# The first sequence normalized in groups of one, one and two token tiles, and the first nine loads on one queue

## The chip, the cores and the metric

The kernel runs on one core of a Trainium2 chip. A core has a matrix engine (TensorE, PE in the profile), a vector engine (VectorE, DVE), a scalar engine (ScalarE, ACT), a general engine (GpSimd, POOL) and a sync engine (SyncE, SP) that here only issues transfers between the device memory and the on-chip buffers. Each engine works through its own list of instructions in order and waits for the others by semaphores. The metric is the time of one execution in device microseconds, lower is better; it is given as the median of several runs.

## The reference, cut to what matters

Four sequences of 512 tokens with 256 features pass through a gated linear scan ("attention") and then through six feed-forward blocks. The computation is in float32.

```python
def _layernorm(x, axis=-1, eps=1e-05):
    m = jnp.mean(x, axis=axis, keepdims=True)
    v = jnp.var(x, axis=axis, keepdims=True)
    return (x - m) / jnp.sqrt(v + eps)

def _L0_attn_ref(x, Wq1, Wq2, Wk1, Wk2, Wv, Wo, norm_w):
    q = jax.nn.silu(x @ Wq1 @ Wq2)        # 256 -> 128 -> 512
    log_f_raw = x @ Wk1 @ Wk2             # 256 -> 128 -> 512
    v = x @ Wv                            # 256 -> 512
    f = jax.nn.sigmoid(log_f_raw)
    a = jnp.exp(jax.nn.log_sigmoid(f))
    k = 1.0 - a
    _, h = jax.lax.associative_scan(combine, (a, k * v), axis=1)   # h_t = a_t h_(t-1) + k_t v_t
    out = q * h
    out = out * jax.lax.rsqrt(jnp.mean(out * out, axis=-1, keepdims=True) + EPS) * norm_w
    return out @ Wo                       # 512 -> 256

# six blocks, the last without the layer norm behind it
h = jax.nn.gelu(jnp.einsum('bsd,hd->bsh', x, w1) + b1, approximate=False)   # 256 -> 1024
x = jnp.einsum('bsh,dh->bsd', h, w2) + b2 + x                               # 1024 -> 256
x = (x - mu) * jax.lax.rsqrt(var + LN_EPS) * g + b

# the whole
x = L0_attn_x                                             # (4, 512, 256)
x = x + _layernorm(attention(_layernorm(x)))
x = x + _layernorm(ffn(_layernorm(x)))
```

## The kernel before, in words

**Tiles.** A sequence is four token tiles of 128 tokens (rows) by 256 features. The products want the features on the partitions, so a normalized token tile is transposed: for each of the two halves `d` of the 256 features one transpose per token tile. For the first two sequences PE does it against the identity (`transpose`, L547; `to_features`, L714) into one of two PSUM tiles `pt`, which ACT copies to the on-chip memory. The later sequences pass through DRAM instead (`passage`, L748: DVE transposes blocks of 32, SP stores the block, and four reads, L744, bring it back in the other order).

**Stages.** For each sequence: layer norm; features; `k1_q1` (L835), which multiplies by Wk1 and Wq1 to two results of 128 x 512; then for each of four quarters `e` of the 512 value features `value(e)` (L840, the product with Wv) and `scan(e)` (L845: products of `k1` and `q1` with quarters of Wk2 and Wq2, sigmoids on ACT, the scan itself on DVE, the product with q on POOL). The output product of one sequence (`output`) is mixed into the scans of the next. Behind the attention come six feed-forward blocks for two groups of two sequences, whose products are computed from sums of blocks of the weights and inputs that POOL forms.

**The first sequence.** Its tiles are normalized in two groups of two tiles (`first_norm`, L789): statistics on DVE (`token_stats`, L673, two instructions, L678 and L679), an add and a power of -0.5 on POOL for the two tiles together (`rstd_of`, L683, recorded as L520 and L508), then subtract and multiply on DVE (`centred`, L707, recorded as L520). `first_features` (L810) transposes a group's two tiles for each `d` and copies 128 x 256 to the on-chip memory. `projected` (L819) then makes its products group by group, so that k1, q1 and value of the first sequence consist of products with 256 columns each, where later sequences have 512.

**Warming.** Before any data is there, PE multiplies a tile of ones by itself (`warm`, L587) into a PSUM bank that nothing reads: six products of 256 columns at once (`WARM`, L592), and two more of 128 columns (`FILL`, L1292) that are tied to the second normalized tile `one.n[1]`.

**Loads.** The token tiles of the first sequence go out alternately on SP's and ACT's queue (L599), Wk1 and Wv on ACT's, Wq1, Wk2 and Wq2 on SP's. Sequence 1's tiles, the norm weights, Wo, the other sequences and the first feed-forward weights follow on SP's. Transfers take their completion semaphores from a set of eight in turn, so a transfer waits until the one eight places before it has landed.

**Order.** Nothing but the start (the warming products, the constants) is issued in the order of the text. Each operation is recorded with an engine, an estimated cost and its dependencies (`Plan.op`, L269). `Plan.latest` (L290) gives each one a due time, counted back from the end along PE's work, and `Plan.run` (L308) simulates the engines: each takes, of what is ready by the estimated times, the operation that is due first. The order that comes out is fixed in the program. A change in costs or dependencies at the start can thus shift the order on any engine further on.

Of the kernel before, what the change touches and what calls it, by code (L numbers as in the profile page):

```python
# [16 lines left out]
P = 128  # L17
# [9 lines left out]
POOLROWS = (2,)  # L27
AFTER = 6.0
LAST_WAYS = "POOL POOL ACT DVE DVE".split()
WARM = 6  # L30
FILL = 2


# [112 lines left out]
def lines_of(text):  # L146
    return [line.split() for line in text.strip().split("\n")]


class View:  # L150


    def __init__(self, bufs, ap, turns):
        self.bufs, self.ap, self.turns = bufs, ap, turns
# [103 lines left out]
class Plan:  # L258
# [6 lines left out]

    def __init__(self):
        self.ops = []

    def op(self, engine, cost, emit, reads, writes, wire=None):  # L269
        n, deps = len(self.ops), set()  # L270
        for v in (*reads, *writes):
            assert v.turns == tuple(b.turn for b in v.bufs), "taken by another"
        for b in (b for v in reads for b in v.bufs):
            deps.add(b.writer)
            b.readers.append(n)
        for b in (b for v in writes for b in v.bufs):
            deps.add(b.writer)
            deps.update(b.readers)
            b.writer, b.readers = n, []
        self.ops.append((engine, cost, emit, deps - {n, None}, wire))  # L280
# [9 lines left out]
    def latest(self):  # L290

        last = [1e9] * len(self.ops)
        at = sum(cost for engine, cost, *_ in self.ops if engine == "PE")
        end = at + AFTER
        for n in reversed(range(len(self.ops))):
            engine, cost, _, deps, _ = self.ops[n]
            if engine == "PE":
                at = min(at - cost, last[n])
                last[n] = at
            elif last[n] == 1e9:  # L300
                last[n] = end
            for d in deps:
                a = self.ops[d]
                took = a[1] + (2.0 + a[4] if a[4] else 0.0)
                last[d] = min(last[d], last[n] - self.lag(d, n) - took)
        return last

    def run(self):  # L308
# [45 lines left out]
def kernel(  # L354
# [30 lines left out]
    NB, _, HID = w1t.shape  # L385
    NT = S // P
    ND = E // P
# [11 lines left out]
    plan = Plan()  # L399

    def tiles(name, shape, n=1, pool=sb):
        return [
            Buf(pool.tile(shape, F32, tag=f"{name}{k}", name=f"{name}_{k}"))
            for k in range(n)
        ]
# [7 lines left out]
    xs = [[Buf(v.ap[:, ts(t, E)]) for t in range(NT)] for v in x_of]  # L413
# [35 lines left out]
    txs = [Buf(tx_of.ap[:, ts(k, 2 * P)]) for k in range(len(lines_of(B_SUMS)))]  # L449
# [29 lines left out]
    mvs = Ring([tiles(f"mv{k}", [P, NT, 2], 1)[0] for k in range(8)])  # L479
    rs = Ring(tiles("r", [P, 4, NT], 8))  # L480
# [20 lines left out]
    def tt(engine, dst, a, b, alu):  # L501
        cost = 0.14 + 0.00213 * dst.size if engine == "POOL" else 0.07 + 0.00104 * dst.size
        if alu == ALU.pow:
            cost = 0.29 + 0.18 * dst.size
        plan.op(
            engine,
            cost,
            lambda: on(engine).tensor_tensor(dst.ap, a.ap, b.ap, alu),  # L508
            [a, b],
            [dst],  # L510
        )

    def tscalar(engine, dst, src, s0, s1, op0, op1=None):
        by = [s.ap if isinstance(s, View) else s for s in (s0, s1)]
        kw = {} if op1 is None else {"op1": op1}
        cost = 0.15 + 0.003 * dst.size if engine == "POOL" else 0.07 + 0.001 * dst.size
        plan.op(
            engine,
            cost,
            lambda: on(engine).tensor_scalar(dst.ap, src.ap, *by, op0, **kw),  # L520
            [src, *(s for s in (s0, s1) if isinstance(s, View))],
            [dst],
        )
# [23 lines left out]
    def transpose(dst, src):  # L547
        plan.op(
            "PE",
            0.107,  # L550
            lambda: nc.tensor.transpose(dst.ap, src.ap, ident.ap),
            [src],
            [dst],
        )

    def load(dst, src, engine="SP"):
        queue = nc.sync if engine == "SP" else nc.scalar
        kept = isinstance(src, View)
        plan.op(
            engine,  # L560
            0.45,
            lambda: queue.dma_start(out=dst.ap, in_=src.ap if kept else src),
            [src] if kept else [],
            [dst],
            dst.size * P * 4 / 0.26e6,
        )
# [17 lines left out]
    nothing, unread = txs[-1], banks.free[-1]  # L584
    nc.vector.memset(nothing.ap, 1.0)

    def warm(n):  # L587
        nc.tensor.matmul(
            unread.ap[:, :n], nothing.ap[:, :P], nothing.ap[:, :n], start=True, stop=True
        )  # L590

    for _ in range(WARM):  # L592
        warm(2 * P)
# [2 lines left out]
    nc.vector.memset(ones.ap, 1.0)  # L596

    nc.scalar.activation(sts.bufs[0].ap[:, :1], ones.ap, AF.Sigmoid)
    for t in range(NT):  # L599
        load(xs[0][t], x[0, ts(t, P), :], ("SP", "ACT")[t % 2])  # L600
    load(wk1_s, wk1.rearrange("(c p) h -> p c h", p=P), "ACT")
    load(wq1_s, wq1.rearrange("(c p) h -> p c h", p=P))
    load(wv_s, wv.rearrange("(c p) f -> p c f", p=P), "ACT")
    load(wk2_s, wk2)
    load(wq2_s, wq2)

    def load_x(b):
        for t in range(NT):
# [74 lines left out]
    def rstd_of(mv, to, of=None, lo=0, hi=NT, negative=True):  # L683

        ve, r, nm, nb = (to[:, k, lo:hi] for k in range(4))
        if of is None:
            tscalar("POOL", ve, mv[:, lo:hi, 1], LN_EPS, None, ALU.add)
        else:
            tt("POOL", ve, of[:, lo:hi], mv[:, lo:hi, 1], ALU.add)
        tt("POOL", r, ve, neg_half[:, lo:hi], ALU.pow)  # L690
        if not negative:
            return r
        tscalar("POOL", nm, mv[:, lo:hi, 0], -1.0, None, ALU.mult)
        tt("POOL", nb, nm, r, ALU.mult)
        return r, nb
# [11 lines left out]
    def centred(src, mv, r, t, t0):  # L707

        z = nns.next()
        by = mv[:, t, 0:1], r[:, t - t0 : t - t0 + 1]  # L710
        tscalar("DVE", z, src, *by, ALU.subtract, ALU.mult)
        return z

    def to_features(srcs, d, xt, scale=None, bias=None):  # L714


        pt = pts.next()[:, : len(srcs) * P]
        for t, src in enumerate(srcs):
            transpose(pt[:, ts(t, P)], src[:, ts(d, P)])
        if scale is None:  # L720
            act(xt, pt)
        else:
            act(xt, pt, AF.Identity, bias, scale)
# [48 lines left out]
    class Attention:  # L772
# [14 lines left out]
                self.there = passage(self.n, early)  # L787

        def first_norm(self):  # L789
            self.n = []  # L790
            for lo in range(0, NT, 2):
                mv = mvs.next()
                for t in (lo, lo + 1):
                    token_stats(mv, xs[self.b][t], t)
                r = rstd_of(mv, rs.next(), lo=lo, hi=lo + 2, negative=False)
                for t in (lo, lo + 1):
                    self.n.append(centred(xs[self.b][t], mv, r, t, lo))
            self.xt = []

        def features(self, d):  # L800
            xt = tcs.next()
# [5 lines left out]
            if d == ND - 1:  # L807
                early.back(self.there)

        def first_features(self, half):  # L810

            for d in range(ND):
                xt = txs[2 * half + d][:]
                to_features(self.n[2 * half : 2 * half + 2], d, xt)
                if half == 0:
                    self.xt.append([])
                self.xt[d].append(xt)

        def projected(self, w):  # L819

# [460 lines left out]
    att = [Attention(b) for b in range(B)]  # L1281
    att[0].first_norm()
    for e in range(NE):
        tscalar("POOL", wo_s[e], wo_s[e], nw_s[:, e : e + 1], None, ALU.mult)
    att[0].first_features(0)
    att[0].first_features(1)
    for b in range(B):
        one = att[b]
        past = att[b - 1] if b else None
        one.k1_q1()  # L1290
        if b == 0:
            for _ in range(FILL):  # L1292
                plan.op("PE", 0.43, lambda: warm(P), [one.n[1]], [unread])
        if b + 1 < B:
            att[b + 1].norm()
        if b >= 2:
            att[b - 2].ffn_norm(early)
        one.value(0)
        one.scan(0)
        one.value(1)  # L1300
        if past:
            past.output(0)
        one.scan(1)
        if past:
            past.output(1)
        one.value(2)
        if past:
            past.output(2)
        one.scan(2)
        if past:  # L1310
            past.output(3)
        one.value(3)
        if past:
            past.residual()
        if b >= 2:
            att[b - 2].ffn_input(0)
        if b + 1 < B:
            att[b + 1].features(0)
        one.scan(3)
        if b >= 2:  # L1320
            att[b - 2].ffn_input(1)
        if b + 1 < B:
            att[b + 1].features(1)
# [7 lines left out]
    for i in range(NB):  # L1331
        for g in range(NG):
            last, hidden = output, Hidden(i, g)
# [105 lines left out]
```

## Time and profile before

| what | value |
| --- | --- |
| median of 3 runs | 685.31 us (685.26 to 686.22) |
| the profiled execution's own time | 685.2 us |
| its span, first to last instruction | 683.4 us |
| mean granted TensorE clock over the span | 0.998 |
| PE busy | 671.9 us (98%) |
| DVE, ACT, POOL busy | 469.7, 357.8, 531.9 us |
| moved by DMA | 73.74 MB, mean 108 GB/s |
| PE's first matmul | 1.17 us after the span's start |
| PE's first transpose of a normalized tile | 6.68 us |
| PE's last matmul ends | 676.8 us |

The profile shows one execution. A line names an engine, a source line, an operation, output<-inputs by the program's names, the shape, how many (xN), and times; what stands in brackets or behind an arrow is the idle time ahead of it and what ended it. "PE" are matmuls, "PEld" weight loads, which lie beside them. A float32 product appears as two matmul rows. Since many operations are recorded by a helper, one line number can stand for many places: L540 is any product, L551 any transpose, L508 any tensor-tensor operation on DVE or POOL, L491 and L493 activations and copies on ACT. "SPq" and "ACTq" rows are the issue of a transfer, not the transfer.

### The profile page before, as it was taken

The numbers are of one execution on the slowest core, as the hardware profiler recorded it, in microseconds if no ns is written. First come the engines' busy times: TensorE is split into PE (matmuls) and PEld (weight loads), VectorE is DVE, ScalarE is ACT, GpSimd is POOL, SyncE is SP. The second block draws the span as 40 slices with busy tenths as digits, with TensorE's granted clock in tenths as the row PEclk, the third lists the DMA queues.
The fourth block names the chain that finished last, engine by engine and source line by source line (L and its number), as shares of the span: only waits on it lengthen the run. The fifth ranks groups of instructions, "written<-read, shape, count | busy, mean of one in ns | idle before, by whom it ended". The sixth has DMA issues, their size and how long they took to land.

```text
span 683.4 us, 8266 instructions
## 1 busy us (share of the span) xinstructions
PE 671.9 (98%) x2384; PEld 443.6 (65%) x2384; DVE 469.7 (69%) x902; ACT 357.8 (52%) x623; POOL 531.9 (78%) x692
## 2 busy tenths in 40 slices
PE   8999999999999999999999999999999999999995
PEld 7565568747658568467476585584674765855885
DVE  5567666866938839759569478387495694793955
ACT  3847757725734636437257346364472482463731
POOL 4997769858988668996589886589866798875764
PEclk9999999999999999999999999999999999999999
DMA  8401312143262141440431631414514306316511
GB/s 253 165 1 62 123 62 80 45 154 92 88 204 78 55 161 43 181 154 24 153 94 62 216 92 64 151 35 175 162 32 153 93 1 195 112 56 185 153 40 62
DMA packets 81838, 73.74 MB, mean 108 GB/s; under 512 B 6272, under 2 KB 70784, under 8 KB 81792
## 3 DMA queue, kind: packets, MB, share of 16 engines
q1 hardware_dynamic: 80672, 72.02, 32.6%
q10 hardware_dynamic: 1120, 1.18, 0.6%
q8 instruction: 19, 0.31, 0.2%
q14 instruction: 27, 0.22, 0.1%
HBM read 43.82 MB, written 29.36 MB: 107 GB/s over the span
## 4 chain that ended last, share of the span: by engine, by line
PE 66%; DVE 17%; POOL 8%; ACT 4%; issue 4%; DMA 0%; DVEq 0%; POOLq 0%; ACTq 0%
PE bank L540 60%; DVE ht L508 9%; POOL tc L508 5%; PE pt L540 5%; DVE tmp L508 3%; DVE st L678 2%; ACT ht L491 2%; DVE tc L508 1%; ACT tmp L493 1%; POOL tx L508 1%; DVE mv L679 1%; POOL r L508 1%; POOL r L520 1%; ACT bank L491 0%; DMA x<-in_x 0%
## 5 line engine op out<-in xcount | busy, mean ns | idle before, releaser
L540 PE MATMUL bank<-tx,sa 128*128 128x256 f32 x672 | 163.1, 380 | 1.7 <-ACT tmp L493 1.5
L493 ACT COPY tmp<-bank 128x512 f32<-128x512 f32 x144 | 83.8, 583 | 135.9 <-PE bank L540 127.1
L540 PEld LDWEIGHTS bank<-tx,sa 128*128 128x128 f32 x672 | 126.2, 190 | 28.6 <-issue 7.8
L508 POOL TENSOR_TENSOR tc<-ht,tc 128x512 f32<-128x512 f32 x96 | 123.8, 1300 | 26.8 <-ACT bank L491 22.5
L491 ACT ACTIVATE ht<-ht,b 128x512 f32<-128x512 f32 x156 | 106.9, 715 | 12.6 <-DVE ht L508 12.6
L508 DVE TENSOR_TENSOR ht<-tmp,bank 128x512 f32<-128x512 f32 x156 | 101.3, 679 | 17.5 <-ACT tmp L493 12.5
L540 PE MATMUL bank<-tc,w 128*128 128x512 f32 (+1 forms) x216 | 95.2, 578 | 0.0
L508 DVE TENSOR_TENSOR tmp<-tmp,bank 128x512 f32<-128x512 f32 x96 | 64.4, 677 | 40.2 <-PE bank L540 23.3
L540 PE MATMUL bank<-tc,sb 128*128 128x512 f32 (+2 forms) x208 | 88.2, 560 | 0.9
L540 PE MATMUL bank<-ht,sb 128*128 128x512 f32 (+2 forms) x208 | 88.0, 555 | 0.0
L530 DVE SCALAR_TENSOR_TENSOR tmp<-bank,b,xt 128x512 f32<-128x512 f32 (+1 forms) x52 | 36.4, 700 | 74.7 <-PE bank L540 74.7
L540 PE MATMUL bank<-ht,w 128*128 128x512 f32 (+1 forms) x200 | 83.0, 567 | 0.0
L508 POOL TENSOR_TENSOR tx<-xt,tx 128x256 f32<-128x256 f32 x108 | 75.8, 733 | 1.0
L540 PEld LDWEIGHTS bank<-tc,sb 128*128 128x128 f32 x208 | 38.5, 190 | 47.1 <-issue 35.4
L540 PEld LDWEIGHTS bank<-tc,w 128*128 128x128 f32 x216 | 40.7, 190 | 39.9 <-issue 36.1
L508 POOL TENSOR_TENSOR tx<-xt 128x256 f32<-128x256 f32 x24 | 17.4, 727 | 60.0 <-ACT xt L491 50.8
L540 PEld LDWEIGHTS bank<-ht,w 128*128 128x128 f32 x200 | 37.9, 190 | 38.1 <-issue 31.8
L491 ACT ACTIVATE n<-x,r 128x256 f32<-128x256 f32 x90 | 47.7, 587 | 26.7 <-POOL r L508 26.7
L540 PEld LDWEIGHTS bank<-ht,sb 128*128 128x128 f32 x208 | 39.0, 190 | 33.7 <-issue 30.6
L508 DVE TENSOR_TENSOR tmp<-bank,tmp 128x512 f32<-128x512 f32 (+2 forms) x54 | 35.4, 655 | 36.1 <-PE bank L540 27.4
L540 PE MATMUL bank<-tx,w 128*128 128x256 f32 x224 | 56.8, 379 | 0.0
L540 PE MATMUL bank<-xt,w 128*128 128x256 f32 x192 | 51.4, 379 | 0.0
(94 smaller groups left out, 1019.2 us busy)
## 6 DMA issues: line engine op xcount, KB each, us to landing
x<-passed SPq DMA_DIRECT2D x120, 128.0 KB, 2.9
passed<-x SPq DMA_DIRECT2D x16, 512.0 KB, 2.7
passed<-x SPq DMA_DIRECT2D x28, 256.0 KB, 2.5
room<-passed SPq DMA_DIRECT2D x56, 128.0 KB, 3.1
w<-in_w1t SPq DMA_DIRECT2D x6, 1024.0 KB, 5.0
w<-in_w2t SPq DMA_DIRECT2D x6, 1024.0 KB, 5.7
passed<-room SPq DMA_DIRECT2D x16, 256.0 KB, 2.2
passed<-room SPq DMA_DIRECT2D x6, 512.0 KB, 2.7
```

The lines of the kernel that those rows point to most:

```text
L491: lambda: nc.scalar.activation(dst.ap, src.ap, func, **kw)
L493: else nc.scalar.copy(dst.ap, src.ap),
L508: lambda: on(engine).tensor_tensor(dst.ap, a.ap, b.ap, alu),
L520: lambda: on(engine).tensor_scalar(dst.ap, src.ap, *by, op0, **kw),
L530: lambda: nc.vector.scalar_tensor_tensor(dst.ap, a.ap, by, b.ap, op0, op1),
L540: lambda: nc.tensor.matmul(dst.ap, lhs.ap, rhs.ap, start=start, stop=True, skip_group_check=True),
L678: nc.vector.bn_stats(st.ap, src.ap)
L679: nc.vector.bn_aggr(mv.ap[:, t, :], st.ap)
```

## The change

The norm and features of the first sequence go in groups of one, one and two tiles; the products of its first two tiles have 128 columns each instead of 256 for both. The fillers hang on the first normalized tile instead of the second. There are five warming products instead of six. The first nine loads all go out on SP's queue, in an order that is written down (their due times are set to very early values, in that order), and no load is left on ACT's queue.

```diff
-WARM = 6
+WARM = 5
+FIRST = ((0,), (1,), (2, 3))
 FILL = 2
@@ class Plan
     def __init__(self):
         self.ops = []
+        self.first = 0
@@ latest
                 last[d] = min(last[d], last[n] - self.lag(d, n) - took)
+        last[: self.first] = [n - 1e9 for n in range(self.first)]
         return last
@@ loads
-    for t in range(NT):
-        load(xs[0][t], x[0, ts(t, P), :], ("SP", "ACT")[t % 2])
-    load(wk1_s, wk1.rearrange("(c p) h -> p c h", p=P), "ACT")
-    load(wq1_s, wq1.rearrange("(c p) h -> p c h", p=P))
-    load(wv_s, wv.rearrange("(c p) f -> p c f", p=P), "ACT")
-    load(wk2_s, wk2)
-    load(wq2_s, wq2)
+    firsts = [
+        (xs[0][0], x[0, ts(0, P), :]),
+        (xs[0][1], x[0, ts(1, P), :]),
+        (wk1_s, wk1.rearrange("(c p) h -> p c h", p=P)),
+        (wq1_s, wq1.rearrange("(c p) h -> p c h", p=P)),
+        (xs[0][2], x[0, ts(2, P), :]),
+        (xs[0][3], x[0, ts(3, P), :]),
+        (wv_s, wv.rearrange("(c p) f -> p c f", p=P)),
+        (wk2_s, wk2),
+        (wq2_s, wq2),
+    ]
+    for dst, src in firsts:
+        load(dst, src)
+    plan.first = len(firsts)
@@ first_norm
-            self.n = []
-            for lo in range(0, NT, 2):
-                mv = mvs.next()
-                for t in (lo, lo + 1):
+            self.n, self.xt = [], [[] for _ in range(ND)]
+            for group in FIRST:
+                mv, lo = mvs.next(), group[0]
+                for t in group:
                     token_stats(mv, xs[self.b][t], t)
-                r = rstd_of(mv, rs.next(), lo=lo, hi=lo + 2, negative=False)
-                for t in (lo, lo + 1):
+                r = rstd_of(mv, rs.next(), lo=lo, hi=group[-1] + 1, negative=False)
+                for t in group:
                     self.n.append(centred(xs[self.b][t], mv, r, t, lo))
-            self.xt = []
@@ first_features
-        def first_features(self, half):
-            for d in range(ND):
-                xt = txs[2 * half + d][:]
-                to_features(self.n[2 * half : 2 * half + 2], d, xt)
-                if half == 0:
-                    self.xt.append([])
-                self.xt[d].append(xt)
+        def first_features(self):
+            for k, group in enumerate(FIRST):
+                for d in range(ND):
+                    xt = txs[ND * k + d][:, : len(group) * P]
+                    to_features([self.n[t] for t in group], d, xt)
+                    self.xt[d].append(xt)
@@ the start of the program's body
-    att[0].first_features(0)
-    att[0].first_features(1)
+    att[0].first_features()
...
-                plan.op("PE", 0.43, lambda: warm(P), [one.n[1]], [unread])
+                plan.op("PE", 0.43, lambda: warm(P), [one.n[0]], [unread])
```

## The prediction

> **What bounds the kernel now.** I read the page first, then the waits of TensorE, the chain of waits in order of time, and the timeline of the first 14 us. The page:
>
> ```profile
> PE 671.9 (98%) x2384; PEld 443.6 (65%) x2384; DVE 469.7 (69%) x902; ACT 357.8 (52%) x623; POOL 531.9 (78%) x692
> ```
>
> TensorE (PE) is busy for all but 11.5 us of 683.4, so the time is its start, its work, its few gaps and a tail. The waits of PE over the span show the two gaps of the start (1.2 us, then 0.6 us for the first normalized tile):
>
> ```profile
> PE bank L588 <- DVE ones L596: 1.2, 1, 1.2
> PE pt L551 <- DVE n L520: 0.6, 1, 0.6
> ```
>
> The same view from 8 to 168 us has no row, and PE's busy time there is 160.00 of 160 us. So whatever lets PE's real work begin earlier, at unchanged work, shortens the whole run one for one, as long as no wait appears behind it. The chain says what the beginning hangs on: the second token tile's load, then its statistics, the reciprocal root on POOL, the normalized tile:
>
> ```profile
> 1.19 3.20 DMA x<-in_x
> 5.45 0.74 POOL r L508
> 6.21 0.42 DVE n L520
> 6.68 0.76 PE pt L551 x4
> 8.89 15.08 PE bank L540 x58
> ```
>
> In the timeline (start, duration), see when each step starts and how long one takes:
>
> ```profile
> 1.17 4.93 PE L588 MATMUL bank<-tx 128*128 128x256 f32 x12 [1.17 <-DVE ones L596]
> 2.89 0.43 DVE L678 BATCH_NORM_STATS2 st<-x 128x6 f32<-128x256 f32 x1 [1.75 <-DMA x<-in_x]
> 4.41 0.43 DVE L678 BATCH_NORM_STATS2 st<-x 128x6 f32<-128x256 f32 x1 [0.88 <-DMA x<-in_x]
> 4.60 0.38 ACTq L562 DMA_DIRECT2D w<-in_wv  x1
> 5.14 0.23 POOL L520 TENSOR_SCALAR r<-mv 128x2 f32<-128x2 f32 x1 [3.85 <-DVE mv L679]
> 5.45 0.73 POOL L508 TENSOR_TENSOR r<-r,neg_half 128x2 f32<-128x2 f32 x1
> 6.21 0.74 DVE L520 TENSOR_SCALAR n<-x,mv,r 128x256 f32<-128x256 f32 x2
> 7.28 0.61 PE L588 MATMUL bank<-tx 128*128 128x128 f32 x4
> 7.37 0.65 ACT L493 COPY tx<-pt 128x256 f32<-128x256 f32 x2 [5.16 <-PE pt L551]
> 11.70 1.03 POOL L508 TENSOR_TENSOR r<-r,neg_half 128x4 f32<-128x4 f32 x1
> 13.48 1.88 PE L540 MATMUL bank<-tc,w 128*128 128x512 f32 x4
> ```
>
> My mark is that last row, PE's first 512-column products (the first scan, e = 0): before it lie all warming, transposes, k1, q1 and value(0).
>
> **The change, part by part.** Each product appears as two PE rows. A row of 256 columns starts 216 ns after the one before it; a row of 128 columns 111.5 ns (the fillers at 7.28; a transpose 109 or more). The first rows are slower: 427 ns apart up to the one that starts at 5.17, 216 ns from the one at 5.50.
>
> *Warming.* Five products are ten rows; the next row can start at 5.50. The removed one cost nothing, since PE then waited 0.6 us.
>
> *First tile.* x tile 0 is still the first load: statistics at 2.89, aggregate over at 3.53. POOL's add takes 0.23. The power takes 0.73 on two columns, 1.03 on four, so about 0.58 on one (estimate; 0.73 at most): 3.93 to 4.51. VectorE's (DVE's) order in the compiled program puts tile 1's statistics before n0, so tile 1 must land by about 3.9 not to delay n0 (4.53 to 4.94). PE is not free before 5.50; n0 may be half a microsecond late for nothing.
>
> *The loads.* SP now issues all nine, some 0.47 us apart: tile 1 at 1.16, wk1 1.6, wq1 2.1, tiles 2 and 3 at 2.6 and 3.1, wv 3.6. Before, ACT's queue held wv until 4.60. From issue to the first use took tile 0 2.17 us, alone in front; the 14 x loads on SP have a median of 3.2 us. The lower end gives tiles 1, 2, 3 at 3.3, 4.8, 5.3, the upper 4.4, 5.8, 6.3. I take 3.5, 4.9, 5.4: nothing else fills the 16 DMA engines now, so tile 0's row is the nearest.
>
> *Second tile.* Statistics of tile 2 stand before n1 on DVE: 4.96 to 5.59 with the aggregate; POOL's second root is ready by 5.5; n1 5.62 to 6.03.
>
> *Tiles 2 and 3.* Tile 3's statistics stand behind n1: 6.05 to 6.66; POOL 6.75 to 7.78 (0.23 and 0.73 on two columns); n2 to 8.22, n3 to 8.63. That is 0.6 us later than now (n3 ends at 7.99): the price of the new order, on PE's path only if PE runs dry.
>
> *PE.* Transposes of n0 from 5.50, four filler rows to 6.28, n1's transposes to 6.5 (their PSUM tiles are copied out at 6.42, with about 0.27 us for a 128-column copy by the rows 0.37 for 256 and 0.58 for 512; 0.37 would cost 0.15). k1 and q1 of tiles 0 and 1: 16 rows, 6.55 to 8.33. One wv product (needs wv by 8.33; issue to landing was 4.6 us for wv now, so 8.2 at worst from that row) to 8.56. Transposes of n2 at 8.56, of n3 at 8.67 to 8.90. Eight wv rows to 9.79, covering the copies (to 9.8). k1 and q1 of tiles 2 and 3, eight 256-column rows: 11.53. wv: 12.39. Two of those rows belong to value(1), so the mark compares at 12.17 against 13.48: 1.31 us earlier. The 22 split rows still to come cost 22 x (111.5 - 108) ns = 0.08. **Sum: 1.23 us.**
>
> With the upper end of the landings n1 ends at 6.86 and n3 at 9.5, and the mark compares at 13.02: gain 0.4. With no wait at all behind 5.50 the rows add up to 6.55 us, the mark is 12.05: gain 1.35.
>
> *Clock.* The switch of pace came 4.0 to 4.3 us after PE's first matmul; five warming products cover just 4.33 us. If it came later, n0's transposes, fillers and first products would run at half pace, losing about half of each late microsecond; before, the sixth product and the wait hid this up to 6.7. The Trainium skill (TensorE: Matmul & The Clock Gate, "Part 1: The HAM clock gate") says that the gate opens after sustained activity, judged in a free-running window, so its moment shifts by some 500 ns from run to run. By that rule up to 0.4 us of cold rows could fall behind 5.50, and the sum would be 1.0 rather than 1.23.
>
> *SP and POOL behind.* Sequence 1's loads follow the nine: from about 5.0, 0.47 apart, instead of 3.12 and 5.2 to 7.0. DVE takes their statistics when n3 is done (8.63); four at 0.6 us end at 11.1, as now (POOL took them up at 11.38). Their readers, ACT's normalizations at 16.18, come later still. One more root (0.8 us on POOL) falls where POOL idles until 5.14. The Trainium skill (DMA: Bandwidth & Descriptors, "Issuing engines are not separate DMA queues") says that several issuing engines share the same DMA engines and save only issue time; that is what this change gives up, and by that rule the loads would land no sooner on one queue. Tiles 2 and 3 do pay it (issued at 2.6 and 3.1, now 1.16 and 1.60), and it is in the sum.
>
> *The order later.* The planner's new times reshuffle ACT, DVE and POOL as far as the first FFN block; PE's order changes at k1/q1 of the last sequence and in the first FFN steps only. The tightest place I find is sequence 3's passage through DRAM:
>
> ```profile
> 66.06 0.32 SPq L575 DMA_DIRECT2D passed<-tx  x1
> 68.67 2.53 SPq L744 DMA_DIRECT2D tx<-passed  x4
> 71.30 0.55 SPq L575 DMA_DIRECT2D passed<-tx  x1
> 75.30 1.12 ACT L493 COPY tc<-tx 128x512 f32<-128x512 f32 x2
> ```
>
> In the new order its normalization stands behind three ACT operations, its store comes some 2 us later (68.1), and its reads stand on SP behind sequence 0's store. I get the reads at 70.7 to 73.2, landed near 76 (2.6 to 3.5 us), copies over at 78.3 and 78.9. PE, which asked at 76.77, now does five output products first (5 x 0.432 = 2.16 us): 78.93 and 79.36. It fits with 0.4 us to spare: price 0 (from 0 to some 0.5 by the landing spread).
>
> The profiled execution took 685.2 us (span 683.4), 0.1 below the median of 685.31; less 1.2 that is 684.0, and by the median **684.1**.
>
> **Rivals.** *A: the start gains less*, because the loads land at the slow end or the clock rises late: 0.2 to 0.8 us gained, 684.5 to 685.1. For it: two x loads on one queue became usable far apart (2.89 and 4.97); against it, ACT's queue competed then. *B: slower, by the passage.* SP issues in order: if sequence 0's store waits for its normalization, sequence 3's reads wait behind it, and PE idles at k1. Each microsecond past the 0.4 is lost whole; store at 74.0 instead of 70.5 leaves PE waiting 1.7 us (685.8), and from 2.6 us on (store at about 75) the kernel is over 0.2% slower, around 687. For it: POOL, whose root the store hangs on, is busy 20.00 of 20 us from 28 to 48 and 15.84 of 20 from 48 to 68; against it, the store would have to be 4 us later than I count. *C: no change*: the new tile order makes PE run dry at n2 by as much as it won, 685.3; against it, there are 1.8 us of first-half products to fill the time.
>
> **How the numbers follow.** Base case 0.55 (683.6 to 684.5), A 0.22, B 0.15, C 0.08. Some 0.2% (1.4 us) is what a measurement of this kernel can tell from no change, and the base case sits just inside it: the runs before spread from 685.26 to 686.22, mean 685.60, against which 684.1 is 0.22%. So I give faster 0.40 (nearly three quarters of the base case), same 0.43 (the rest, A, C and the mild part of B), slower 0.17 (B and reshuffles that I don't see). Range 683.4 (full gain and 0.5 us of spread) to 686.6, which takes in A, C and half of B; the base case alone is 683.6 to 684.5.
>
> **What would show it.** Right: n0's transposes near 5.5 us with no wait of PE before them, the first 512-column row near 12.4, n3 near 8.6, no PE wait from 9 to 168 us. Wrong: the first slow rows reaching past 6 us, PE waiting for wv or n2, or a PE wait at k1 of the last sequence (77 to 79 us).

## The result

The changed kernel takes 686.71 us (median of 21 runs, 686.18 to 687.99), the kernel before 685.49 us (21 runs beside it, 684.85 to 686.22). The ratio is 1.0019, 95% interval 1.0013 to 1.0026: slower by 1.2 us, where 684.1 was forecast, faster by 1.2. The profiled execution took 686.18 us, its span 684.4 (before 685.2 and 683.4); the mean granted clock is 0.998 in both.

### The profile page after: what moved, and what is told of

Same layout as the page of the kernel before. It is cut to its first block, busy times and chain, and to the rows that moved or that the text cites. A ratio compares the mean times of both kernels' runs of the same rounds, so it can differ in the third digit from the quotient of the medians.

```text
span 684.4 us, 8315 instructions
## 1 busy us (share of the span) xinstructions
PE 672.1 (98%) x2406; PEld 443.9 (65%) x2406; DVE 469.6 (69%) x902; ACT 358.4 (52%) x625; POOL 532.6 (78%) x694
## 4 chain that ended last, share of the span: by engine, by line
PE 63%; DVE 20%; POOL 8%; ACT 5%; issue 4%; DMA 0%; SPq 0%; DVEq 0%; POOLq 0%
PE bank L543 58%; DVE ht L511 10%; POOL tc L511 6%; PE pt L543 5%; DVE tmp L511 3%; DVE st L689 3%; ACT ht L494 2%; ACT tmp L496 1%; DVE tc L511 1%; DVE mv L690 1%; POOL r L511 1%; POOL r L523 1%; ACT bank L494 0%; ACT n L494 0%; DMA x<-in_x 0%
## 5 line engine op out<-in xcount | busy, mean ns | idle before, releaser
L543 PE MATMUL bank<-tx,w 128*128 128x256 f32 (+1 forms) x240 | 57.3, 365 | 0.0
```

The lines of the kernel that those rows point to most:

```text
L543: lambda: nc.tensor.matmul(dst.ap, lhs.ap, rhs.ap, start=start, stop=True, skip_group_check=True),
```

## The profile after

The page's line of busy times of the changed kernel:

```profile
PE 672.1 (98%) x2406; PEld 443.9 (65%) x2406; DVE 469.6 (69%) x902; ACT 358.4 (52%) x625; POOL 532.6 (78%) x694
```

PE has 22 more rows (the split products) and the same busy time within 0.2 us. So the extra microsecond is not work. The waits of PE from 0 to 170 us, same kernel (who waited <- for whom: us in all, how often, the longest):

```profile
PE bank L591 <- DVE ones L599: 1.2, 1, 1.2
PE bank L543 <- POOL tc L511: 1.0, 1, 1.0
PE bank L543 <- DVE tmp L511: 0.5, 1, 0.5
PE pt L554 <- DVE n L523: 0.2, 1, 0.2
```

The first and the last row answer to the two rows of the kernel before: the wait for the first normalized tiles fell from 0.6 to 0.2 us. The two in the middle are new. Before, there was no PE wait from 8 to 168 us at all.

The start itself is close to the forecast. Rows of the timeline (start, duration):

```profile
5.42 0.43 DVE L689 BATCH_NORM_STATS2 st<-x 128x6 f32<-128x256 f32 x1 [0.46 <-DMA x<-in_x]
5.45 0.38 PE L554 MATMUL pt<-ident,n 128*128 128x128 f32 x2
5.98 0.38 DVE L523 TENSOR_SCALAR n<-x,mv,r 128x256 f32<-128x256 f32 x1
6.51 0.41 PE L554 MATMUL pt<-ident,n 128*128 128x128 f32 x2 [0.23 <-DVE n L523]
12.69 1.88 PE L543 MATMUL bank<-tc,w 128*128 128x512 f32 x4
```

The first transposes run at 5.45 (before 6.68). The second normalized tile stands on DVE behind the third tile's statistics, whose load lands only at 5.4, and so PE waits 0.23 us for it. The mark, the first 512-column row, is at 12.69; two rows of value(1) lie before it, so it compares at 12.47 with 13.48. Less 0.08 us for the split rows still to come that is 0.93 us ahead. PE's later products keep this lead: one at 48.90 us in the kernel before starts at 47.97 in this one, one at 118.71 at 117.78.

From there the lead is lost twice over. The chain of waits in order of time (start, duration, what it consists of), changed kernel:

```profile
117.21 0.72 ACT ht L494
...
120.51 0.48 ACT tmp L496
...
121.02 0.70 DVE tmp L511
...
121.76 15.99 PE bank L543 x58
...
137.78 0.55 POOL r L523
138.33 1.25 POOL tc L511
...
139.62 2.41 PE bank L543 x5
```

From 99.7 to 116.1 us this chain consists of PE alone. Then it goes through ACT's first four gelus and the copies between them to a sum on DVE (`tmp`), for which PE waits until 121.76; and at 137.78 through POOL, where the first step of a reciprocal root (`r`) and then the sum `tc` that PE needs are done. With the pauses around them, PE loses 0.74 us at 121, 0.2 at 131 and 1.29 at 139, 2.2 us in all. Against the lead of 0.93 that is 1.3; the spans differ by 1.0. The 0.3 comes back from 446 to 453 us, where the kernel before waits 0.46 us in two small waits and this one 0.16 in one.

POOL takes `r` ahead of `tc` in the kernel before as well, so that order is not what is new at 139. What is new is when POOL comes to the sums. In the changed kernel:

```profile
130.72 1.88 DVE L511 TENSOR_TENSOR ht<-tmp,bank 128x512 f32<-128x512 f32 x3 [0.98 <-ACT tmp L496]
135.07 2.62 POOL L511 TENSOR_TENSOR tc<-ht,tc 128x512 f32<-128x512 f32 x2 [4.40 <-DVE tc L511]
```

and in the kernel before (there `r` runs at 136.59):

```profile
133.99 2.51 POOL L508 TENSOR_TENSOR tc<-ht,tc 128x512 f32<-128x512 f32 x2 [3.05 <-DVE tc L508]
137.11 1.27 POOL L508 TENSOR_TENSOR tc<-ht,tc 128x512 f32<-128x512 f32 x1
```

There the sum is over at 138.38 and PE takes it at 138.42, without a wait. In the changed kernel POOL comes to the two sums 1.1 us later, held up by DVE, and DVE has waited 0.98 us for a copy on ACT (130.12) that stands behind ACT's gelus. PE itself began the products ahead of these sums at about the same time in both (131.46 and 131.55).

Why is ACT late at 117? The timeline of the changed kernel:

```profile
111.52 0.23 POOL L523 TENSOR_SCALAR r<-mv 128x4 f32<-128x4 f32 x1
112.40 0.21 POOL L511 TENSOR_TENSOR r<-r 128x4 f32<-128x4 f32 x1
112.64 1.58 ACT L494 ACTIVATE n<-room,r 128x256 f32<-128x256 f32 x3 [1.33 <-POOL r L511]
115.91 1.28 ACT L494 ACT_TABLE_LOAD   x1
117.21 0.72 ACT L494 ACTIVATE ht<-ht,b 128x512 f32<-128x512 f32 x1
```

and of the kernel before:

```profile
101.33 0.23 POOL L520 TENSOR_SCALAR r<-mv 128x4 f32<-128x4 f32 x1
101.64 0.20 POOL L508 TENSOR_TENSOR r<-r 128x4 f32<-128x4 f32 x1
104.02 1.09 ACT L491 ACTIVATE n<-room,r 128x256 f32<-128x256 f32 x2
112.25 1.28 ACT L491 ACT_TABLE_LOAD   x1
114.31 1.33 ACT L491 ACTIVATE ht<-ht,b 128x512 f32<-128x512 f32 x2 [0.78 <-DVE ht L508]
```

`r` and `n` here are the attention norm of the third sequence (`residual`). Its last two small POOL operations (together 0.4 us) are issued 10 us later than before, behind POOL's sums of the feed-forward inputs. ACT's four normalizations (2.2 us) hang on them and slide from 104 to 107 us to 112.6 to 115.3; the load of ACT's table and the first gelu stand behind. Before, the table load fell into a stretch in which ACT had nothing to do (it waited another 0.78 us for its input afterwards). Now DVE has made the inputs of the first two gelus from 112.67 to 113.95, and the first gelu starts only at 117.21.

## The experiments

The theory is that the later order costs the time: the planner, given other times at the start, deals the work of ACT, DVE and POOL out differently, and the start itself is a gain. The rival "too early" is that PE simply arrives sooner at work that ACT and POOL can't finish sooner, in whatever order. A third is that the start loses somewhere that the profile doesn't show.

The planner's costs are numbers in the program, used only for the order. So the order can be changed without changing an instruction. This made two kernels with start and order crossed.

**New start, old order.** On the changed kernel:

```diff
-                plan.op("PE", 0.43, lambda: warm(P), [one.n[0]], [unread])
+                plan.op("PE", 1.0, lambda: warm(P), [one.n[0]], [unread])
```

> The change complete, but its planner reckons a filler at 1.0 us instead of 0.43 us. No instruction differs; from about 60 us on every engine issues in the order of the kernel before (one of the two fillers also falls behind k1 and q1 of the first two tiles). Theory 'order' (the later order causes the loss): no PE gap at 121, 131 and 138 us, the start's gain is kept less 0.22 us for the moved filler: 684.5 to 684.9 us, about 0.7 us under the kernel before. Rival 'too early' (PE arrives 0.9 us sooner at work that ACT and POOL have not done, in whatever order): the gaps are there again with about 0.7 to 1 us together, and the time is that of the kernel before, 685.3 to 685.8 us. Third, 'something in the start itself' (loads, clock): as the changed kernel, 686.5 us or more.

Measured: 685.13 us (684.53 to 686.49) beside 685.53 for the kernel before, ratio 0.9993 (0.9985 to 1.0002). Its PE waits up to 170 us:

```profile
PE bank L591 <- DVE ones L599: 1.2, 1, 1.2
PE pt L554 <- DVE n L523: 0.5, 1, 0.5
```

The two middle rows are gone, at nearly the same start. The median is 1.6 us below that of the changed kernel, at 0.4 us under the kernel before instead of the 0.7 expected; the interval takes in no gain at all. The profiled execution, 684.53, is 0.7 us under that of the kernel before.

**Old start, new order.** On the kernel before, the cost of the first transposes:

```diff
-            0.107,
+            0.107 if len(plan.ops) > 200 else 0.02,
```

> The kernel before, but its planner reckons the first transposes at 0.02 us instead of 0.107 us. No instruction differs and the start is the old one; behind the first 60 instructions every engine issues in exactly the order of the changed kernel. Theory 'order': PE waits at about 122, 132 and 139.5 us for some 2.2 us in all, and with no gain at the start the kernel takes 687.3 to 687.9 us, the slowest of all. Rival 'too early': PE comes 0.9 us later to the same places, so most of the waits are gone and the time is at most that of the changed kernel, 685.6 to 686.7 us.

Measured: 687.36 us (686.54 to 687.85), ratio 1.0024 (1.0015 to 1.0032). PE's waits up to 170 us:

```profile
PE bank L588 <- DVE ones L596: 1.2, 1, 1.2
PE bank L540 <- POOL tc L508: 1.0, 1, 1.0
PE bank L540 <- DVE tmp L508: 0.5, 1, 0.5
```

Both waits are there at the same length (0.474 and 1.022 us, against 0.473 and 1.023), at 121.97 and 139.29, although PE comes 0.7 us later. "Too early" falls: nothing is gained by arriving later. Since ACT and POOL themselves wait for PE's earlier products, the whole pattern moves with PE. The cost 0.02 holds for the transposes among the first 200 recorded operations, those of the first two sequences. By the traces, the engines issue in the changed kernel's order from 41 us on (SP has one transfer at another place, at 70 us), and in the kernel above in the order of the kernel before from 53 us on. The four corners, each against the kernel before that ran beside it:

| | old order | new order |
| --- | --- | --- |
| old start | 0 | +1.83 us |
| new start | -0.40 us | +1.22 us |

The order costs 1.6 to 1.8 us with either start, which is clear of the intervals. The start gains 0.4 to 0.6 us with either order, which is not: each interval reaches about half a microsecond to either side. (The new start with the old order has one filler behind k1 and q1, so its corner is not quite the changed kernel's start.)

**The named step alone.** On the changed kernel, two due times (`rstd_of` in `residual`, the last two operations of the third sequence):

```diff
+        for n, by in self.shift.items():
+            last[n] += by
         return last
...
             by = rstd_of(self.mv, rs.next(), of=ve)
+            if self.b == 2:
+                plan.shift = {n: -4 for n in range(len(plan.ops) - 2, len(plan.ops))}
```

> The change complete with its start and its PE order; only the due time of two small POOL operations (the -mean and -mean/deviation of the third sequence's attention norm, issued at 111.52 and 112.40 us) is set 4 us earlier. Theory 'order, and in it this step': ACT normalizes that sequence some 5 us sooner and loads its table in an idle stretch, the gap of 0.47 us at 121.3 goes (0.74 us with the restart) and, as POOL's later sums move too, the one at 138.6 (1.3 us) as well: 684.4 to 685.0 us. If this step only causes the first gap: 685.8 to 686.1 us. If the waits have another cause: 686.5 us or more with both gaps.

Measured: 684.57 us (684.22 to 685.46), ratio 0.9983 (0.9974 to 0.9991), 2.1 us below the changed kernel and faster than the kernel before. The timeline, rows that answer to those above:

```profile
107.12 0.23 POOL L526 TENSOR_SCALAR r<-mv 128x4 f32<-128x4 f32 x1
109.23 0.20 POOL L514 TENSOR_TENSOR r<-r 128x4 f32<-128x4 f32 x1
112.16 1.28 ACT L497 ACT_TABLE_LOAD   x1
113.51 0.72 ACT L497 ACTIVATE ht<-ht,b 128x512 f32<-128x512 f32 x1
```

The first gelu starts 3.7 us earlier than in the changed kernel, and PE has no wait from 6.6 to 167 us. PE's order is the same as in the changed kernel; of the others only ACT, DVE and POOL behind 107 us moved. The sums that PE had waited for at 139 are made in time:

```profile
133.21 2.51 POOL L514 TENSOR_TENSOR tc<-ht,tc 128x512 f32<-128x512 f32 x2 [3.83 <-DVE tc L514]
136.33 1.27 POOL L514 TENSOR_TENSOR tc<-ht,tc 128x512 f32<-128x512 f32 x1
```

POOL still does `r` (135.81) ahead of the last of them; it comes to them 1.9 us earlier than in the changed kernel, and ACT's copy before them stands behind one gelu less. So 0.4 us of POOL work, put behind sums that nobody needed yet, is what the loss begins with. That both waits go with it is shown; the path from it to the second wait is read from the rows, and no run takes away one of the two waits alone.

**Fillers on the second tile.** On the changed kernel:

```diff
-                plan.op("PE", 0.43, lambda: warm(P), [one.n[0]], [unread])
+                plan.op("PE", 0.43, lambda: warm(P), [one.n[1]], [unread])
```

> The change complete, but the two fillers stay tied to the second normalized tile, as before. The later order is then nearly that of the kernel before. PE waits from 5.7 us for the second tile (0.45 us more idle than in the changed kernel) and does the fillers behind it. Theory 'order': no gap at 121 and 138 us, the start's gain falls from 0.93 to about 0.5 us: 684.8 to 685.2 us. If the start itself loses (fillers needed, clock falling back in the idle time): 685.5 us or more without gaps behind 120 us. Rival 'too early': 685.3 to 685.8 us with some of the gaps.

Measured: 685.35 us (684.62 to 686.52), ratio 0.9995 (0.9986 to 1.0003). PE waits 1.1 us for the second tile and not at all from 7 to 168 us; the order is nearly that of the kernel before. The gain of 0.2 us is less than expected, and its interval takes in none. The fillers' edit, which moves 0.45 us of filling at the start, thus belongs to what tips the order: the rest of the change without it has none of the two waits. It does not tip it alone: the groups with the fillers' edit, but with the loads as before, have none of them either (the run on the groups below).

**The loads alone** (groups of two, six warming products, fillers as before):

```diff
-WARM = 5
-FIRST = ((0,), (1,), (2, 3))
+WARM = 6
+FIRST = ((0, 1), (2, 3))
...
-                plan.op("PE", 0.43, lambda: warm(P), [one.n[0]], [unread])
+                plan.op("PE", 0.43, lambda: warm(P), [one.n[1]], [unread])
```

> Only the loads' part of the change: nine loads on one queue in the new order; groups of two tiles, six warming products and the fillers on the second tile as before. The later order is that of the kernel before. Theory: PE's first transposes at about 6.1 to 6.4 us (before 6.68), but with the third and fourth tile landing at 5.4 to 5.7 us (before 4.6 to 4.9) their normalized tiles come at 8.1 to 8.5 us and PE, which has only one product in front of their transposes, waits about 1 us for them: 685.1 to 685.6 us, a gain of 0 to 0.4 us, with no gaps at 121 and 138 us. If the loads are what gains: 684.6 us or less.

**The groups alone** (the loads on two queues as before):

```diff
-    for dst, src in firsts:
-        load(dst, src)
-    plan.first = len(firsts)
+    for t in range(NT):
+        load(xs[0][t], x[0, ts(t, P), :], ("SP", "ACT")[t % 2])
+    load(wk1_s, wk1.rearrange("(c p) h -> p c h", p=P), "ACT")
...
```

> Only the groups' part of the change: groups of one, one and two tiles, five warming products, fillers on the first tile; the loads on two queues as before. The later order is that of the kernel before. Theory: the first transposes at about 6.0 us, the second at about 7.2, as Wk1 lands only at 7.2 us the products of k1 start at 7.3 to 7.5 us (before 7.96): 685.0 to 685.5 us, a gain of 0 to 0.5 us. If the groups are what gains: 684.6 us or less.

Measured: loads alone 685.78 us (685.36 to 687.01), ratio 1.0005 (0.9996 to 1.0014); groups alone 685.97 us (685.01 to 688.57), ratio 1.0010 (0.9998 to 1.0022). Neither gains; both lie above what was expected, and neither is clear of no change. With the loads alone, the third tile's statistics, whose load comes late, stand on DVE in front of the first normalized tile (5.74) and the fourth's in front of the second (6.69):

```profile
5.18 0.43 DVE L689 BATCH_NORM_STATS2 st<-x 128x6 f32<-128x256 f32 x1 [1.06 <-DMA x<-in_x]
```

In this profile PE also stayed slow until 7.3 us, later than in any other: its first transposes, at 6.45, stood behind slow warming rows and not behind a load. With the groups alone, the first statistics on DVE start at 3.7 us (2.9 in the changed kernel), the statistics of a third tile again stand ahead of the first normalized one, and PE runs dry for 1.5 us:

```profile
3.73 0.43 DVE L682 BATCH_NORM_STATS2 st<-x 128x6 f32<-128x256 f32 x1 [2.60 <-DMA x<-in_x]
6.74 0.44 PE L554 MATMUL pt<-ident,n 128*128 128x128 f32 x2 [1.46 <-DVE n L523]
```

The kernel before, with the same loads, had its first statistics at 2.89, so the 0.8 us of their delay are a late landing in this one execution and not the groups. Neither part showed a gain without the other; the two profiles give reasons for it that are in part those of a single execution.

**The second normalized tile before the third tile's statistics.** On the kernel of the named step, a planner-only operation that makes the third tile's statistics come after `n[1]` on DVE:

```diff
+            order = lambda *r: plan.op("DVE", 0.0, lambda: None, r[:-1], [r[-1]])
...
+                if lo == 2:
+                    order(self.n[1], xs[self.b][2])
                 for t in group:
                     token_stats(mv, xs[self.b][t], t)
```

> As the run with the two POOL operations early, and VectorE forms the second normalized tile before the statistics of the third tile instead of behind them (only the order of VectorE and, by the planner, of a few wv products and transposes at the start moves; later orders are identical). If the start's missing third of a microsecond is the second tile's wait for the third tile's load (PE gap 0.41 us at 6.1 in that run): PE's second transposes at 5.8 to 6.0 us instead of 6.53, no gap before them, the first 512-column row at 12.2 to 12.4 instead of 12.79, 684.0 to 684.3 us. Rival: PE then reaches wv before it has landed (7.84 us in the changed kernel) and waits there as long: 684.5 to 684.8 us.

**And the token tiles loaded first** (the pairs of Wk1, Wq1 and of tiles 2, 3 change places in `firsts`):

> As e5, and the four token tiles are loaded ahead of Wk1 and Wq1. Every other order is that of e5. If a token tile's landing still holds the start in e5: third tile's statistics directly behind the second normalized tile and up to 0.3 us less, 683.8 to 684.2 us. If Wk1 and Wq1 are then late (issued 0.95 us later; they landed at 4.20 and 4.64 us, PE asks at about 6.0 and 6.9): no difference up to 0.3 us more, 684.0 to 684.6 us.

Measured: 684.46 us (683.52 to 685.25), ratio 0.9982 (0.9973 to 0.9991), and 684.39 us (683.68 to 685.57), ratio 0.9985 (0.9976 to 0.9994). Both are 0.1 to 0.2 us under the run of the named step, less than their intervals can tell. The first lies between the two ranges expected, the second in the range for no difference. In both PE had no wait for the second tile and none for Wv, but in the first one's profile its transposes still came only at 6.79:

```profile
5.59 0.63 PE L557 MATMUL pt<-ident,n 128*128 128x128 f32 x2
6.02 0.93 PE L594 MATMUL bank<-tx 128*128 128x128 f32 x4
6.79 0.38 PE L557 MATMUL pt<-ident,n 128*128 128x128 f32 x2
```

The first transposes and the fillers ran at half pace: four filler rows took 0.93 us here and 0.61 in the changed kernel. Ready data was met by a slow PE, which the expectation had not reckoned with.

**Warming.** Four products instead of five on the kernel with the tiles first, and six instead of five on the kernel of the named step:

```diff
-WARM = 5
+WARM = 4
```

> As the run with the token tiles loaded first, with four warming products instead of five. The first normalized tile is ready at 5.0 us and the second at 5.9 us there, while ten warming rows ended at 5.6 us and the fillers at 6.3 us. If TensorE's change of pace comes at its own moment (4.5 to 7.1 us in the profiles so far): first transposes at 5.0 to 5.2 us, second at about 5.9 us instead of 6.29, 684.0 to 684.3 us. If the pace changes later for want of warming work, the 36 rows of 128 columns behind run slow for as long: 684.5 to 684.9 us.

```diff
-WARM = 5
+WARM = 6
```

> As the run with the two POOL operations early, with six warming products as before the change. The prediction's step: the removed product cost nothing and its removal gains nothing by itself. Ten rows ended at 5.29 us there, and PE then had 0.41 us of waiting for the second tile in front of its transposes at 6.53. Two more rows take 0.43 us at the fast pace: second transposes at 6.5 to 6.6 us, the same time within 0.15 us, 684.5 to 684.7 us. If the rows are slow (0.85 us for two) or the wait is shorter: up to 0.5 us more, 685.0 us. If the sixth product brings a better clock: less than 684.3 us.

Measured: 684.32 us (683.88 to 685.45), ratio 0.9985 (0.9976 to 0.9994), and 684.65 us (683.95 to 686.08), ratio 0.9990 (0.9981 to 0.9999). Against the kernel before that ran beside each, one product more or less changes the time by 0.1 to 0.2 us, which is not told from nothing. Six products came out as expected; four just above the range for the better case. With four, this profile again shows slow rows and then a wait for Wv (0.37 us), which the earlier k1 and q1 reach before it has landed:

```profile
5.59 1.06 PE L594 MATMUL bank<-tx 128*128 128x128 f32 x4
...
9.13 0.94 PE L546 MATMUL bank<-tx,w 128*128 128x128 f32 x6 [0.37 <-DMA w<-in_wv]
```

Five of these kernels (the named step, the same with six products, the second tile first, the tiles loaded first, and that with four products) beat both the kernel before and the changed one, by 0.7 to 1.2 us and by 2.0 to 2.4 us. Among themselves they can't be told apart.

## Why the prediction was wrong

The step that failed is "The order later": it said that the planner's new times reshuffle ACT, DVE and POOL as far as the first FFN block, looked for the tightest place, took sequence 3's passage and gave the whole reshuffle the price 0. At the passage it was right: PE waited nowhere from 76 to 79 us. But the loss is 40 us further on, at 121 and 139 us, in the block whose order it had itself named as changed, and it is 2.2 us in the profile and 1.6 to 1.8 us in the medians. What the runs showed in place of the price 0: two small POOL operations of the third sequence moved back by 10 us, and with them the first gelus; setting the due times of these two alone takes away both waits and 2.1 us. The chance of slower, 0.17, lay mostly on a mechanism (rival B, SP's order) that didn't occur; reshuffles not seen had only what was left of it.

The rows for it were in the profile of before. ACT's idle time from 108 to 114.3 us was 0.34, 0.28, 1.14 and 0.78 us, about 2.5 us, around a table load that held nobody up. The longest of the four, ahead of the load:

```profile
111.86 0.37 ACT L493 COPY room<-pt 128x256 f32<-128x256 f32 x1 [1.14 <-PE pt L540]
```

Four normalizations (2.2 us) that come later than 107 us have to go into this idle time, and if their root is ready only at 112.6 they push the table load and the first gelu ahead of them. The prediction looked for the place with the least slack and did not ask which operations had moved furthest: the two on POOL, by 10 us.

Point by point, the other steps:

- *Warming*: forecast that the next PE row can start at 5.50 and that the removed product costs nothing. Seen 5.45; six products instead of five made 0.1 to 0.2 us, not told from nothing. Right.
- *First tile*: n0 forecast from 4.53 to 4.94; seen 4.55 to 4.96. Right.
- *The loads*: tiles 1, 2, 3 taken as usable at 3.5, 4.9 and 5.4. Tile 1's statistics started at 3.46, but tile 2's at 5.42 behind a DMA wait of 0.46 us. This is the term that was mis-sized: n1 came at 5.98 instead of 5.62, and the mark at 12.69 instead of 12.39. It is within the bounds given (5.8 for tile 2). Rival A's reading that a second load on SP was usable only at 4.97 is not what the row says: DVE took those statistics up at 4.97 straight behind others, without a wait for the load.
- *Tiles 2 and 3*: n2 and n3 done at 8.80 against 8.63, with no PE wait for them. Right, and rival C falls.
- *SP and POOL behind*: sequence 1's statistics began at 10.67 behind a DMA wait of 1.87 us, where 8.63 was forecast (7.91 before). No one needed them sooner; price 0 was right.
- *The sum*: 1.23 us forecast, 0.93 us in the profile, 0.4 to 0.6 us in the medians of the crossed kernels. By these the start did what rival A said (0.2 to 0.8 us); but with the named step put right the same start is 0.96 us under the kernel before, and the intervals do not tell the two apart.
- *Clock*: taken as nothing, with 0.2 us by the page. In the profiled execution it cost nothing (the change came at 5.3 us); over many executions it is more, by the estimate in the last section.

What the prediction named as signs of being wrong were slow rows past 6 us and a PE wait for wv or n2 or at k1 of the last sequence. None of these came in the changed kernel's profile; "no PE wait from 9 to 168 us" was the right thing to look at, and it failed at 121.

## What to carry to other kernels

Where a planner or scheduler sets the order, an edit at the start is two edits: its own, and the order that comes out of the new times. List what moved on each engine, take what moved furthest (here two small POOL operations by 10 us), follow its readers to the next thing that PE waits for, and set the sum of what is pushed against the idle time there; and measure the two apart by crossing them, since a cost that only the planner reads changes the order without changing an instruction. A lead of PE is only worth what no later wait takes back.

## What was not expected of the hardware

PE changes from slow rows (427 ns for 256 columns, 213 for 128) to fast ones (216 and 110) at very different moments. Worked out from the row that holds the change in each of the twelve profiles, it came at 4.5, 4.6, 4.9, 5.0, 5.3, 5.4, 5.7, 6.7, 6.7, 6.8, 6.9 and 7.3 us, always with PE's first matmul at 1.17; the kernel before was at 5.4 and the changed one at 5.3. With early change (fillers on the second tile, ten warming rows in 4.05 us):

```profile
1.17 4.05 PE L591 MATMUL bank<-tx 128*128 128x256 f32 x10 [1.17 <-DVE ones L599]
```

and with late change (six warming products, twelve rows without one fast among them; two slow transposes take 0.61 us after them):

```profile
1.17 5.49 PE L594 MATMUL bank<-tx 128*128 128x256 f32 x12 [1.17 <-DVE ones L602]
```

The windows of the profile list a granted clock of 1.00 from 1 to 8 us even where the rows are slow. The trace's own record of the clock begins at the change: its first entry lies at the moments given above in all twelve, within 0.1 us, and ahead of it there is none, which the view shows as 1.00. So the mean clock of 0.998 leaves the slow start out, and the start has to be read from the rows. The Trainium skill (TensorE: Matmul & The Clock Gate, "Part 1: The HAM clock gate") puts the change at around 4 us of sustained matmul activity, within 500 ns from run to run. Counted from the first matmul it came here 3.3 to 6.1 us in, a spread of 2.8 us; the measurement decides.

An estimate of what this does, from these twelve moments: rows that matter begin at about 5.3 us in the new start and at 6.6 in the old one, and each microsecond by which the change comes after them costs half of itself, since the rows take twice as long. That is 0.35 us on the mean for the new start and 0.06 for the old one. It could account for some 0.3 us of the difference between the start's gain in the profile (0.93, with a change at 5.3) and in the medians (0.4 to 0.6), a difference that the intervals alone would allow too. This was argued from the rows and not tried. What sets the moment stays open: it did not follow the number of warming products (eight rows: 6.7; ten: 4.5 to 6.7; twelve: 5.4 to 7.3).

A smaller one: in two profiles (the groups alone, the second tile first) PE waited 0.63 and 0.61 us at 200 us for POOL, behind a copy on ACT that waited for a passage's read from DRAM (ACT's waits for these reads from 190 to 201 us: 11.5 us in both, 10.0 us with the tiles loaded first). The other profiles don't have this wait. So the landing of single transfers far behind the start may be a part of the spread between executions of one kernel (1.2 to 3.6 us here); this was not tried.
